# VectorE's work on the FFN input goes ahead of the rows between up and down, with two loads moved

## The chip, the cores and the metric

The kernel runs on one NeuronCore of a Trainium2 chip. The metric is device time in microseconds (us) of one execution. The engines that matter here are TensorE (PE), VectorE (DVE), ScalarE (ACT), GpSimd (POOL), and SyncE (SP), which issues nearly all DMAs. Each takes its instructions in the order in which the program lists them.

## The reference

The input x has 8 sequences of 1024 rows of 512 float32 numbers. One transformer layer is computed, in float32:

```
x1  = x  + attention(layernorm(x))      # 16 heads, low-rank queries, keys and values, rotary part, causal
out = x1 + ffn(layernorm(x1))
ffn(y) = down( silu(gate(y)) * up(y) )  # 512 -> 1408 -> 512
```

Each of the three linear maps of the FFN first rounds its input and its weights to a 4-bit grid: in blocks of 16 numbers, divided by the block's largest magnitude / 6, rounded to 0, 0.5, 1, 1.5, 2, 3, 4 or 6, and multiplied back. So `y` (the normalised x1) is rounded before gate and up, and `h = silu(gate) * up` before down.

## The kernel before

**Units and tiles.** The rows are cut into 16 units of 512 rows (two for each sequence) and each unit into 4 tiles of 128 rows, 64 tiles in all. Attention runs unit by unit: four groups of four heads, each with 3 (even units) or 7 (odd units) score steps. A score step is a set of score matmuls into the PSUM tile `sc_ps`, of which there is one, two exponentials on ScalarE (L597), a clamp of one half on VectorE (L612) and of the other on GpSimd (L615), masks on GpSimd (L619), and, one step later on PE, the matmuls with the values into `num`. VectorE also adds up the weights of the steps (L641). After a unit's attention comes the output projection (`po`), to which VectorE adds x (L772, tile `xo`); the sum x1 goes to a DRAM tile `mid`.

**The FFN as filler.** From the fifth unit on, pieces of the FFN are laid between the score steps, of tiles whose x1 has been stored. For tile n the pieces are: `fetch(n)` (load x1 into `y`, L786), `begin(n)` (layer norm and rounding of y, on VectorE), `turned(n)` (PE turns y, L212, and ScalarE copies it into `yT`), `gate(n, 0..2)` and `up(n, 0..2)` (chunks of 512, 512 and 384 columns), and `down(n)` (11 matmuls into `pd`). `down(n - 2)` stands between gate and up of tile n. For most of the kernel the pattern repeats every two units, that is every ten tiles, about 522 us; below, a tile's type is its number's last digit. The last tiles run after all attention has ended.

**Rows between up and down.** ScalarE copies gate's sums into a tile `h` (L142; two buffers), applies silu, and VectorE multiplies by up's sums (L831). `quantize` then makes the passes that round h: the largest magnitude of each block (L254), six small instructions for the scales (L259 to L264), and for each chunk L281 (divide), L289 and L292 (find the step), L295 twice (round), L277 (multiply back) and a transpose of blocks (L218). These passes are called rows below. Then 16 DMAs on SP (`move_blocks`, L230) put the blocks into `hT` (one buffer), which `down` reads. The y of a tile gets the same passes without the transpose, from 128x512 numbers. The tiles `y`, `sc`, `rs` (scales) and `m` (step) have one buffer each.

**PSUM banks.** All PE results but `sc_ps` and `num` go through three banks in turn (`bank`, pool `ps_t`): gate's and up's `pg`, the turned y `pt`, `pd`, `po`, and the projections `pp`, `pr`, `pf`, `pk`, `pq`, `pqr`, `pv`, `den`. A bank is written again when ScalarE or VectorE has read it.

**Order.** The Python code keeps a model clock (`Clock`) and writes the order of PE, VectorE, ScalarE and SP by it. VectorE's work that is not urgent goes into two queues, `soon` (attention) and `later` (FFN), and `fill` lays jobs from them where the model has VectorE idle before an instruction that waits for PE or ScalarE. `need(key)` lays everything in a queue up to the last job with that key: `turned(n)` needs y of n, `gate(n, 0)` needs h of n - 2. `later` is first in, first out, so y of tile n + 1 comes after whatever of h stands there. DMAs held in `sent` go out when the model clock passes their time or when they are asked for; stores ask before each `fetch`.

```
def gate(n, k):
    if k == 0:
        clk.need(("h", n - 2))
        clk.sent_by_now(("h", n - 2))
        hs[n] = p2.tile([P, FF], F32, tag="h", name="h")
```

Of the kernel before, what the change touches and what calls it, by code (L numbers as in the profile page):

```python
# [11 lines left out]
F32 = mybir.dt.float32  # L12
U32 = mybir.dt.uint32
AF = mybir.ActivationFunctionType
ALU = mybir.AluOpType
# [3 lines left out]
P = 128  # L19
B, S, D = 8, 1024, 512  # L20
# [7 lines left out]
NDC = D // P  # L28
NFC = FF // P
BLK = 16  # L30
# [12 lines left out]
def tile_mla_then_fp4_ffn(  # L43
# [17 lines left out]
    nc = tc.nc  # L61
    const = ctx.enter_context(tc.tile_pool(name="const", bufs=1))
    p1 = ctx.enter_context(tc.tile_pool(name="p1", bufs=1))
# [15 lines left out]
    class Clock:  # L79
# [4 lines left out]
        soon, later = deque(), deque()  # L84
# [14 lines left out]
                job[1]()  # L99

        def lay(self, q):
            cost, run, _, ready = q.popleft()
            self.dve = max(self.dve, ready) + cost
            run()

# [36 lines left out]
        on_act(0.1 + 0.0009 * src.free_size(), lambda: nc.scalar.copy(dst, src))  # L142

    def slack(cost, run, key, soon=False, ready=0.0):
        (clk.soon if soon else clk.later).append((cost, run, key, ready))

    ident = const.tile([P, P], F32, name="ident")
    make_identity(nc, ident)
# [68 lines left out]
    def turn_blocks(part, key, soon=False):  # L217
        slack(0.72, lambda: nc.vector.transpose(part, part), key, soon)  # L218
# [24 lines left out]
    BY_PE = (4 * 2 * B - 1,)  # L243


    def quantize(q, width, key):
        nb = width // BLK
        q3 = q.rearrange("p (b k) -> p b k", k=BLK)
        got = {}

        def amax():
            got["sc"] = sc = p1.tile([P, 88], F32, tag="sc", name="sc")[:, :nb]
            got["rs"] = rs = p1.tile([P, 88], F32, tag="rs", name="rs")[:, :nb]
            nc.vector.tensor_reduce(rs, q3, AX.X, ALU.max, apply_absolute_value=True)  # L254

        def scales():
            sc, rs = got["sc"], got["rs"]

            nc.vector.tensor_scalar(sc, rs, 1.0 / 6.0, None, ALU.mult)  # L259
            nc.vector.scalar_tensor_tensor(rs, sc, -4.0, rs, ALU.mult, ALU.add)  # L260
            nc.vector.scalar_tensor_tensor(rs, sc, -2.0, rs, ALU.mult, ALU.add)
            nc.vector.scalar_tensor_tensor(sc, rs, 1.0 / 6.0, sc, ALU.mult, ALU.add)
            nc.vector.tensor_scalar(sc, sc, 1e-12, None, ALU.max)
            nc.vector.reciprocal(rs, sc)  # L264

        slack(0.06 + 0.0011 * width, amax, key)
        slack(1.1 + 0.008 * nb, scales, key)
        for o in range(0, width, 512):
            step = min(512, width - o)
            part, bl = q[:, o : o + step], slice(o // BLK, (o + step) // BLK)  # L270
            nbl = step // BLK
            part3 = part.rearrange("p (b k) -> p b k", k=BLK)

            def times(which, part3=part3, bl=bl, nbl=nbl):
                by = got[which][:, bl].unsqueeze(2).to_broadcast([P, nbl, BLK])
                if which == "sc":
                    nc.vector.tensor_tensor(part3, part3, by, ALU.mult)  # L277
                else:


                    nc.vector.scalar_tensor_tensor(  # L281
                        part3, part3, BELOW_ONE, by, ALU.mult, ALU.mult
                    )

            def steps(part=part, step=step):
                got["m"] = m = p1.tile([P, 512], F32, tag="m", name="m")[:, :step]
                nc.vector.tensor_scalar(  # L289
                    m.bitcast(U32), part.bitcast(U32), EXP_MASK, None, ALU.bitwise_and  # L290
                )
                nc.vector.tensor_scalar(m, m, 1.0, MAGIC, ALU.max, ALU.mult)  # L292

            def to_grid(op, part=part):
                nc.vector.tensor_tensor(part, part, got["m"], op)  # L295

            pass_cost = 0.06 + 0.00125 * step
            slack(pass_cost, lambda f=times: f("rs"), key)
            slack(1.2 * pass_cost, steps, key)
            slack(pass_cost, lambda f=to_grid: f(ALU.add), key)  # L300
            slack(pass_cost, lambda f=to_grid: f(ALU.subtract), key)
            slack(pass_cost, lambda f=times: f("sc"), key)
            if key[0] == "h" and key[1] not in BY_PE:
                turn_blocks(part, key)


    def weight_pieces():
# [45 lines left out]
    def normed(xt, key):  # L353
        got = {}

        def stats():
            pool, tag = (small, "nx") if key[0] == "x" else (p1, "ny")
            own = pool.tile([P, 10], F32, tag=tag, name=tag)
            st, ve = own[:, 0:6], own[:, 8:9]
            got["mv"], got["rstd"] = mv, rstd = own[:, 6:8], own[:, 9:10]  # L360
            nc.vector.bn_stats(st, xt)
            nc.vector.bn_aggr(mv, st)
            nc.vector.tensor_scalar(ve, mv[:, 1:2], EPS, None, ALU.add)
            nc.gpsimd.tensor_tensor(rstd, ve, neg_half, ALU.pow)

        def scaled():
            nc.vector.tensor_scalar(
                xt, xt, got["mv"][:, 0:1], got["rstd"], ALU.subtract, ALU.mult
            )

        return [(0.9, stats, key), (0.5, scaled, key)]

    def begin_norms(jobs, soon=False):

        parts = [normed(*job) for job in jobs]
        for k in range(2):
            for part in parts:
                slack(*part[k], soon)
# [399 lines left out]


    tiles = [(u, t) for u in range(2 * B) for t in range(NT)]  # L780
    ys, hs, ends = {}, {}, {}

    def fetch(n):
        clk.sent_by_now("store")
        ys[n] = p1.tile([P, D], F32, tag="y", name=f"y_{n}")
        nc.sync.dma_start(out=ys[n], in_=mids[tiles[n]])  # L786

    def begin(n):
        begin_norms([(ys[n], ("y", n))])
        quantize(ys[n], D, ("y", n))  # L790

    def hidden(n, w, off, width):
        pg = bank("pg")[:, :width]
# [9 lines left out]

    def turned(n):
        clk.need(("y", n))
        yT = p2.tile([P, NDC, P], F32, tag="yT", name="yT")
        turn(ys[n], yT, NDC)
        ys[n] = yT

# [32 lines left out]
    def hidden_turned(n, done=None):  # L842

        if n in BY_PE:
            return
        if n > 0 and n - 1 not in used:
            waits[n] = clk.dve
            return
        h = hs.pop(n)

        def make():
            clk.sent_by_now("store")
            ends[n] = p3.tile([P, D], F32, tag="xo", name=f"xr_{n}")
            nc.sync.dma_start(out=ends[n], in_=mids.pop(tiles[n]))
            hTs[n] = p1.tile([P, NFC, P], F32, tag="hT", name="hT")
            return hTs[n]

        move_blocks(h, make, ("h", n), clk.dve if n == 0 or done is None else max(done, clk.pe))

    def down(n):  # L860
        clk.need(("h", n))
        if n in BY_PE:
            ends[n] = p3.tile([P, D], F32, tag="xo", name=f"xr_{n}")
            nc.sync.dma_start(out=ends[n], in_=mids.pop(tiles[n]))
            hTs[n] = p1.tile([P, NFC, P], F32, tag="hT", name="hT")
            for off, width in FCH:
                f0, c = off // P, width // P
                turn(hs[n][:, off : off + width], hTs[n][:, f0 : f0 + c, :], c)
            hs.pop(n)
        else:  # L870
            arrived(("h", n))
        hT = hTs[n]
        pd = bank("pd")
        for i in range(NFC):
            mm(pd, lhsT=hT[:, i, :], rhs=wd_T[:, i, :], start=(i == 0), stop=(i == NFC - 1))
        hTs.pop(n)
        used.add(n)
        if n + 1 in waits:
            hidden_turned(n + 1, waits.pop(n + 1))
        xt = ends.pop(n)  # L880
        on_dve(0.7, clk.pe + 0.3, lambda: nc.vector.tensor_tensor(xt, pd, xt, ALU.add))
        u, t = tiles[n]
        b, rows = rows_of(u, t)
        clk.send(clk.dve, lambda: nc.sync.dma_start(out=out[b, rows, :], in_=xt), "store")

    def ffn_pieces():

        last = len(tiles) - 1
        yield 4.0, 0, lambda: fetch(0)
        yield 10.0, 0, lambda: begin(0)  # L890
        yield 1.0, 0, lambda: turned(0)
        for n in range(last + 1):
            for k in range(3):
                yield (3.4, 3.4, 2.6)[k], n, lambda n=n, k=k: gate(n, k)
                if k < 2 and n < last:
                    yield 0.0, n + 1, lambda n=n, f=(fetch, begin)[k]: f(n + 1)
            if n > 1:
                yield 9.9, n, lambda n=n: down(n - 2)
            for k in range(3):
                yield (3.4, 3.4, 2.6)[k], n, lambda n=n, k=k: up(n, k)  # L900
                if k == 1 and n < last:
                    yield 0.5, n + 1, lambda n=n: turned(n + 1)
        for n in (last - 1, last):
            yield 9.9, last, lambda n=n: down(n)

# [135 lines left out]
```

## Time and profile before

| | |
|---|---|
| median of 3 runs | 3835.66 us (3835.64 to 3838.62) |
| profiled execution: time, span | 3835.01 us, 3833.3 us |
| mean granted TensorE clock | 0.974 |
| busy: PE, DVE, ACT, POOL | 3559.1 (93%), 2873.8 (75%), 1145.5 (30%), 651.2 (17%) us |
| PE's matmuls of gate, up, down | 630.6, 669.2, 622.9 us |

How to read it: PE, DVE and so on are busy times of one profiled execution. A group of instructions is named by the line that records it, so that all matmuls carry L129, and what distinguishes them is the tile they write: `pg`, `pd`, `pt` and so on. A 128x512 matmul appears as two instructions. A wait is listed as who waited, for whom, the total, the number of times and the longest. In a timeline, a row has its start, its length, engine, line, operation, tiles, sizes, the number of instructions, and in brackets the idle time before it with what ended it. A clock of 1.00 or 0.50 is the TensorE clock that was granted in a stretch.

### The profile page before, as it was taken

Reading aid. Unit: us, or ns where it says so; the run is one execution under the profiler, and the core shown is the slowest. Engines: PE = TensorE matmul, PEld = TensorE weight load, DVE = VectorE, ACT = ScalarE, POOL = GpSimd, SP = SyncE. Lnnn points to the kernel's source line nnn. Section 1 sums busy time; section 2 is a strip of 40 time slices with the busy share of each in tenths; the row PEclk is TensorE's granted clock in tenths of the full one; section 3 lists DMA queues with packets and bytes.
Section 4 is the critical chain, followed back from the end, with each engine's and each line's share of the span. In section 5 each row is a group of like instructions: output and inputs, shape, how many; then the busy total and the mean of one; then the engine's idle time right before and its main releaser. Section 6 shows DMA issues by size and latency. Waiting matters only on the chain. (4 is left out here: it accounts for less than half of the span.)

```text
span 3833.3 us, 45944 instructions
## 1 busy us (share of the span) xinstructions
PE 3559.1 (93%) x17119; PEld 1551.5 (40%) x17119; DVE 2873.8 (75%) x5024; ACT 1145.5 (30%) x1473; POOL 651.2 (17%) x838
## 2 busy tenths in 40 slices
PE   6998989999999998999999999989999999998898
PEld 3333334443444443344434444433444344433343
DVE  5886937777878777777778687776878786777776
ACT  2343433332323222232323233322323222232210
POOL 2233321111111111111111111111211111111100
PEclk9999999999999999999999999999999999999999
DMA  3212211311122211222111222112221113211221
GB/s 76 64 37 69 81 36 30 76 38 38 38 63 46 70 38 32 54 56 69 38 38 38 69 54 59 34 32 70 47 68 31 38 38 75 51 41 29 46 61 40
DMA packets 577038, 192.47 MB, mean 50 GB/s; under 512 B 514864, under 2 KB 515888, under 8 KB 576816
## 3 DMA queue, kind: packets, MB, share of 16 engines
q1 hardware_dynamic: 568512, 187.36, 21.0%
q10 hardware_dynamic: 8304, 2.18, 0.3%
q8 instruction: 136, 2.23, 0.2%
q14 instruction: 86, 0.70, 0.1%
HBM read 94.72 MB, written 33.55 MB: 33 GB/s over the span
## 5 line engine op out<-in xcount | busy, mean ns | idle before, releaser
L597 ACT ACTIVATE pT<-sc_ps 128x1024 f32<-128x1024 f32 (+1 forms) x640 | 566.1, 936 | 1174.6 <-PE sc_ps L129 964.6
L129 PE MATMUL pg<-wu_T,yT 128*128 128x512 f32 (+1 forms) x1536 | 669.2, 584 | 3.8 <-DVE xo L772 3.8
L129 PE MATMUL pg<-wg_T,yT 128*128 128x512 f32 (+1 forms) x1536 | 630.6, 561 | 0.7 <-ACT yT L214 0.7
L129 PE MATMUL pd<-wd_T,hT 128*128 128x512 f32 x1408 | 622.9, 598 | 4.4 <-DVE rs L264 4.4
L615 POOL TENSOR_SCALAR pT<-pT 128x1024 f32<-128x1024 f32 (+1 forms) x320 | 342.1, 1069 | 1065.4 <-ACT pT L597 847.6
L619 POOL TENSOR_SCALAR_AFFINE_SELECT pT<-pT 128x256 f32<-128x256 f32 (+1 forms) x384 | 233.4, 608 | 1462.6 <-DVE pT L612 1184.0
L641 DVE TENSOR_TENSOR pT<-pT 128x1024 f32<-128x1024 f32 (+3 forms) x528 | 472.7, 920 | 3.9 <-POOL pT L619 0.6
L129 PEld LDWEIGHTS pg<-wu_T,yT 128*128 128x128 f32 x1536 | 296.9, 200 | 333.9 <-issue 274.4
L129 PEld LDWEIGHTS pg<-wg_T,yT 128*128 128x128 f32 x1536 | 288.8, 190 | 326.1 <-issue 248.9
L129 PEld LDWEIGHTS pd<-wd_T,hT 128*128 128x128 f32 x1408 | 266.3, 191 | 345.5 <-issue 327.6
L612 DVE TENSOR_SCALAR pT<-pT 128x1024 f32<-128x1024 f32 (+1 forms) x320 | 205.0, 641 | 248.0 <-ACT pT L597 246.9
L129 PE MATMUL sc_ps<-qc,kT 32*128 32x512 f32 (+3 forms) x3072 | 343.5, 532 | 9.1 <-ACT pT L597 9.0
L129 PE MATMUL num<-pT,v 128*32 128x512 f32 (+3 forms) x3072 | 326.1, 501 | 5.6 <-POOL pT L619 5.2
L129 PE MATMUL sc_ps<-qr,kr 32*128 32x512 f32 (+3 forms) x3072 | 309.8, 488 | 4.2 <-DVE qr L533 4.2
L142 ACT COPY h<-pg 128x512 f32<-128x512 f32 (+1 forms) x192 | 105.7, 551 | 609.3 <-PE pg L129 580.6
L831 DVE TENSOR_TENSOR h<-pg,h 128x512 f32<-128x512 f32 (+1 forms) x192 | 123.1, 642 | 218.8 <-PE pg L129 208.3
L295 DVE TENSOR_TENSOR h<-h,m 128x512 f32<-128x512 f32 (+1 forms) x384 | 257.3, 670 | 11.8
L129 PE MATMUL po<-wo,aT 128*128 128x512 f32 x512 | 226.2, 600 | 30.9 <-DMA wo<-in_w_o_dram 27.9
L129 PEld LDWEIGHTS sc_ps<-qc,kT 32*128 32x128 f32 x3072 | 115.9, 186 | 226.8 <-issue 154.8
L212 PE MATMUL pt<-ident,y 128*128 128x128 f32 x256 | 48.2, 319 | 168.5 <-DVE y L277 158.1
L772 DVE TENSOR_TENSOR xo<-po,xo 128x512 f32<-128x512 f32 x64 | 44.1, 688 | 202.5 <-DMA xo<-in_x_dram 113.4
L129 PEld LDWEIGHTS sc_ps<-qr,kr 32*128 32x128 f32 x3072 | 147.3, 188 | 109.9 <-issue 85.5
(103 smaller groups left out, 3473.3 us busy)
## 6 DMA issues: line engine op xcount, KB each, us to landing
hT<-h SPq DMA_DIRECT2D x1008, 44.0 KB, 2.1
xo<-in_x_dram SPq DMA_DIRECT2D x64, 256.0 KB, 2.9
wo<-in_w_o_dram SPq DMA_DIRECT2D x16, 1024.0 KB, 5.2
mid<-xo SPq DMA_DIRECT2D x64, 256.0 KB, 2.8
y<-mid SPq DMA_DIRECT2D x64, 256.0 KB, 2.7
xr<-mid SPq DMA_DIRECT2D x64, 256.0 KB, 2.8
out_dram<-xr SPq DMA_DIRECT2D x64, 256.0 KB, 2.0
xp<-in_x_dram SPq DMA_DIRECT2D x30, 512.0 KB, 4.0
```

What stands on the lines that cost most here:

```text
L129: nc.tensor.matmul(dst, **kw)
L142: on_act(0.1 + 0.0009 * src.free_size(), lambda: nc.scalar.copy(dst, src))
L212: nc.tensor.transpose(pt[:, i, :], src[:, i * P : (i + 1) * P], ident)
L295: nc.vector.tensor_tensor(part, part, got["m"], op)
L597: lambda: nc.scalar.activation(part, sc[:, 2 * k : 2 * k + 2, :cols], AF.Exp, scale=SM_SCALE),
L612: lambda: nc.vector.tensor_scalar(part, part, E_HI, E_LO, ALU.min, ALU.max),
L615: nc.gpsimd.tensor_scalar(part, part, E_HI, E_LO, ALU.min, ALU.max)
L619: nc.gpsimd.affine_select(out=diag, in_=diag, pattern=[[0, 2], [0, len(segs)], [1, P]], compare_op=ALU.is_ge, fill=0.0, base=0, channel_mu ...
L641: lambda a=whole, b=part: nc.vector.tensor_tensor(a, a, b, ALU.add),
L772: on_dve(0.7, clk.pe + 0.3, lambda: nc.vector.tensor_tensor(xt, po, xt, ALU.add))
L831: lambda: nc.vector.tensor_tensor(h, pg, h, ALU.mult),
```

## The change

Jobs in VectorE's queues get a fifth field that says whether another tile's passes may be put ahead of them; it is false for the two roundings (L295), since the single tile `m` is in use there. `begin(n)` no longer appends: it puts the layer norm and all rounding passes of y, in one run, at the first place in `later` where that is allowed, so ahead of the rows of h. The scales of y, which so far shared `sc` and `rs` with h, are kept in two stretches of the tile `yT` that y itself will be copied into later. `begin(n + 1)` is called after `gate(n, 0)` and not after `gate(n, 1)`; `fetch(n + 2)` follows `turned(n + 1)`, so that this load stands ahead of `up(n, 2)` and `gate(n + 1, 0)`, where it stood behind both. `turned` sets the model's PE clock to VectorE's if that is later. The load of x1 for the last addition (`xr`) moves from ahead of the 16 moves to `down`. No instruction is added or removed on any engine; the order of PE is the same up to the last two units.

```
-        slack(0.06 + 0.0011 * width, amax, key)
...
+            jobs.append((1.2 * pass_cost, steps, key, True))
+            jobs.append((pass_cost, lambda f=to_grid: f(ALU.add), key, False))
+            jobs.append((pass_cost, lambda f=to_grid: f(ALU.subtract), key, False))
+            jobs.append((pass_cost, lambda f=times: f("sc"), key, True))
...
+    def ahead_of_rows(jobs):
+
+        q = clk.later
+        at = next((i for i, x in enumerate(q) if x[4]), len(q))
+        for job in reversed(jobs):
+            q.insert(at, (*job, 0.0, True))
...
     def begin(n):
-        begin_norms([(ys[n], ("y", n))])
-        quantize(ys[n], D, ("y", n))
+
+        yTs[n] = yT = p2.tile([P, NDC, P], F32, tag="yT", name="yT")
+        jobs = normed(ys[n], ("y", n))
+        scales_in = lambda: (yT[:, 0, : D // BLK], yT[:, 1, : D // BLK])
+        jobs += [x[:3] for x in quantize_jobs(ys[n], D, ("y", n), scales_in)]
+        ahead_of_rows(jobs)
...
     def turned(n):
         clk.need(("y", n))
-        yT = p2.tile([P, NDC, P], F32, tag="yT", name="yT")
+        clk.pe = max(clk.pe, clk.dve)
+        yT = yTs.pop(n)
...
         def make():
-            clk.sent_by_now("store")
-            ends[n] = p3.tile([P, D], F32, tag="xo", name=f"xr_{n}")
-            nc.sync.dma_start(out=ends[n], in_=mids.pop(tiles[n]))
             hTs[n] = p1.tile([P, NFC, P], F32, tag="hT", name="hT")
...
     def down(n):
         clk.need(("h", n))
+        clk.sent_by_now("store")
+        ends[n] = p3.tile([P, D], F32, tag="xo", name=f"xr_{n}")
+        nc.sync.dma_start(out=ends[n], in_=mids.pop(tiles[n]))
...
+        yield 0.0, 1, lambda: fetch(1)
         for n in range(last + 1):
             for k in range(3):
                 yield (3.4, 3.4, 2.6)[k], n, lambda n=n, k=k: gate(n, k)
-                if k < 2 and n < last:
-                    yield 0.0, n + 1, lambda n=n, f=(fetch, begin)[k]: f(n + 1)
+                if k == 0 and n < last:
+                    yield 0.0, n + 1, lambda n=n: begin(n + 1)
...
                 if k == 1 and n < last:
                     yield 0.5, n + 1, lambda n=n: turned(n + 1)
+                    if n + 1 < last:
+                        yield 0.0, n + 2, lambda n=n: fetch(n + 2)
```

More of the change, by code (lines that the diff above doesn't have):

```diff
@@ L101, in lay @@
         def lay(self, q):
-            cost, run, _, ready = q.popleft()
+            cost, run, _, ready, _ = q.popleft()
             self.dve = max(self.dve, ready) + cost
@@ L144, in slack @@
     def slack(cost, run, key, soon=False, ready=0.0):
-        (clk.soon if soon else clk.later).append((cost, run, key, ready))
+        (clk.soon if soon else clk.later).append((cost, run, key, ready, True))
+    def ahead_of_rows(jobs):
[3 more added lines that the diff above has]
+            q.insert(at, (*job, 0.0, True))
     ident = const.tile([P, P], F32, name="ident")
@@ L243, in tile_mla_then_fp4_ffn, with quantize_jobs @@
     BY_PE = (4 * 2 * B - 1,)
-    def quantize(q, width, key):
+    def quantize_jobs(q, width, key, scales_in):
         nb = width // BLK
         q3 = q.rearrange("p (b k) -> p b k", k=BLK)
-        got = {}
+        got, jobs = {}, []
         def amax():
-            got["sc"] = sc = p1.tile([P, 88], F32, tag="sc", name="sc")[:, :nb]
-            got["rs"] = rs = p1.tile([P, 88], F32, tag="rs", name="rs")[:, :nb]
+            got["sc"], got["rs"] = sc, rs = scales_in()
             nc.vector.tensor_reduce(rs, q3, AX.X, ALU.max, apply_absolute_value=True)
@@ L264, in scales @@
             nc.vector.reciprocal(rs, sc)
-        slack(0.06 + 0.0011 * width, amax, key)
-        slack(1.1 + 0.008 * nb, scales, key)
+        jobs.append((0.06 + 0.0011 * width, amax, key, True))
+        jobs.append((1.1 + 0.008 * nb, scales, key, True))
         for o in range(0, width, 512):
@@ L297, in quantize, with own @@
             pass_cost = 0.06 + 0.00125 * step
[L298 to L302, printed above, removed]
-            if key[0] == "h" and key[1] not in BY_PE:
-                turn_blocks(part, key)
+            jobs.append((pass_cost, lambda f=times: f("rs"), key, True))
+            jobs.append((1.2 * pass_cost, steps, key, True))
+            jobs.append((pass_cost, lambda f=to_grid: f(ALU.add), key, False))
+            jobs.append((pass_cost, lambda f=to_grid: f(ALU.subtract), key, False))
+            jobs.append((pass_cost, lambda f=times: f("sc"), key, True))
+            if key[0] == "h" and key[1] not in BY_PE:
+                jobs.append((0.72, lambda p=part: nc.vector.transpose(p, p), key, True))
+        return jobs
+    def quantize(q, width, key):
+        def own():
+            return [p1.tile([P, 88], F32, tag=x, name=x)[:, : width // BLK] for x in ("sc", "rs")]
+        for cost, run, k, free in quantize_jobs(q, width, key, own):
+            clk.later.append((cost, run, k, 0.0, free))
     def weight_pieces():
@@ L780, in tile_mla_then_fp4_ffn @@
     tiles = [(u, t) for u in range(2 * B) for t in range(NT)]
-    ys, hs, ends = {}, {}, {}
+    ys, yTs, hs, ends = {}, {}, {}, {}
     def fetch(n):
@@ L861, in down @@
         clk.need(("h", n))
+        clk.sent_by_now("store")
+        ends[n] = p3.tile([P, D], F32, tag="xo", name=f"xr_{n}")
+        nc.sync.dma_start(out=ends[n], in_=mids.pop(tiles[n]))
         if n in BY_PE:
-            ends[n] = p3.tile([P, D], F32, tag="xo", name=f"xr_{n}")
-            nc.sync.dma_start(out=ends[n], in_=mids.pop(tiles[n]))
             hTs[n] = p1.tile([P, NFC, P], F32, tag="hT", name="hT")
```

## The prediction

> **What bounds the kernel now.** The page comes first: PE is busy 93% of the span, so a change counts by what it does to PE's remaining 270 us of idle time and to the rate at which PE works.
>
> ```profile
> PE 3559.1 (93%) x17119; PEld 1551.5 (40%) x17119; DVE 2873.8 (75%) x5024; ACT 1145.5 (30%) x1473; POOL 651.2 (17%) x838
> ```
>
> Then the list of PE's waits and the cores' clock. The turn of y waits for y's last pass 40 times, 158.1 us in all; no other wait is near it. The turn also waits for L772, the addition of x after the output projection: the bank is late.
>
> ```profile
> PE pt L212 <- DVE y L277: 158.1, 40, 10.0
> PE pt L212 <- DVE xo L772: 10.4, 6, 2.6
> PE pg L129 <- DVE xo L772: 3.8, 4, 1.7
> core 0: 3833.3 us, clock 0.974
> ```
>
> A clock of 0.974 with steps of 0.50 alone means 2 x 0.026 x 3833.3 = 199 us at half rate. The table by windows shows where: behind the waits for y (start and end, length, busy times by engine, clock).
>
> ```profile
> 1941.20:1944.60 3.40, 3.40 (x8) 1.94 (x7) 0.00 (x0) 0.59 (x1) 0.00 (x0) 0.50 0.39 60
> 1989.00:1995.80 6.80, 4.83 (x28) 2.13 (x28) 1.76 (x3) 1.39 (x3) 0.00 (x0) 0.50 0.22 52
> ```
>
> The waits that end at 1940.84 (2.19 us) and 1990.97 (7.37 us) stand just before these. Last, PE's timeline at a tile of type 6 (26), beside ScalarE, VectorE and SP there; the rows of VectorE and SP are the last rows of h of tile 24 and its moves.
>
> ```profile
> 1893.80 1.12 PE L212 MATMUL pt<-ident,y 128*128 128x128 f32 x4 [5.69 <-DVE y L277]
> 1894.70 3.80 PE L129 MATMUL pg<-wu_T,yT 128*128 128x384 f32 x8
> 1898.34 3.60 PE L129 MATMUL pg<-wg_T,yT 128*128 128x512 f32 x8
> 1901.77 1.89 PE L129 MATMUL pp<-xnT,wdq 128*128 128x256 f32 x8
> 1903.59 0.64 PE L129 MATMUL pf<-krp,fold_sb 128*32 128x256 f32 x8
> ...
> 1906.66 1.12 PE L129 MATMUL pqr<-cq,wqr 128*128 128x512 f32 x2
> ```
> ```profile
> 1901.97 0.59 ACT L142 COPY h<-pg 128x512 f32<-128x512 f32 x1 [6.44 <-PE pg L129]
> ```
> ```profile
> 1867.29 0.36 DVE L289 TENSOR_SCALAR m<-h 128x384 uint32<-128x384 uint32 x1
> 1867.68 0.36 DVE L292 TENSOR_SCALAR m<-m 128x384 f32<-128x384 f32 x1
> 1868.08 1.15 DVE L295 TENSOR_TENSOR h<-h,m 128x384 f32<-128x384 f32 x2
> ...
> 1872.02 0.55 DVE L277 TENSOR_TENSOR h<-h,sc 128x384 f32<-128x384 f32 x1
> 1872.60 0.58 DVE L218 STREAM_TRANSPOSE h<-h 128x384 f32<-128x384 f32 x1
> ```
> ```profile
> 1873.31 11.43 SPq L230 DMA_DIRECT2D hT<-h  x16
> ```
>
> The rows of h end at 1873.2, the moves land at 1886.1, and down starts on them at 1916.0: 30 us of slack. In types 0 to 9 this slack is 19 to 50 us. So y is late while h is early.
>
> **What it removes.** I laid VectorE's durations in the changed order, each instruction starting no sooner than the PE, ScalarE or DMA row that it waits for, with PE's rows closed up by the waits removed. y's passes (about 8 us) come one to three score steps sooner, and their last one ends 12 to 55 us ahead of the turn. Only tile 0 is as before: nothing stands between its load and its turn, 9.6 us. Removed: 158.1 - 9.6 = 148.5 us.
>
> L772 waited because the load of x for the projection's second tile stood behind 16 moves on SP; in the new order it stands ahead of them, and PE's 10.4 + 3.8 = 14.2 us go.
>
> ```profile
> 1252.02 10.49 SPq L230 DMA_DIRECT2D hT<-h  x16
> 1262.57 0.60 SPq L182 DMA_DIRECT2D xo<-in_x_dram  x1
> ```
>
> Half clock: between 560 and 3640 us the clock's records have 150.2 us at 0.50, all behind waits for y; 52.6 of them PE was idle anyway (in the second window above 1.97 of 6.80), and 97.6 it worked at half rate, which loses 48.8 us. Gain in all: 148.5 + 14.2 + 48.8 = 211.5 us.
>
> The load of x1 beside down costs nothing: it goes out once SP is past the moves and has 9.6 us of matmuls to land in (2.8 us). y's scales in yT cost nothing: that buffer's last reader, up of the tile two before, is past.
>
> **What it adds: the h buffer.** No instruction is new, but the rows of h now end when `gate(n, 0)` forces them. The row that tells what this costs is ScalarE's wait for the moves, today only in the last tiles:
>
> ```profile
> ACT h L142 <- DMA hT<-h: 19.3, 3, 7.0
> ```
>
> h has two buffers, so the copy of gate's first chunk of tile n must wait until the moves have read h of n - 2. Type 6 by the rows above: up's last chunk ends on PE at 1898.5, its product (L831, 0.56) at 1899.1; in the new order a whole last chunk of h follows, 0.36 + 0.36 + 1.15 + 0.55 + 0.58 = 3.0, to 1902.1. Sixteen moves at 0.65 us and 2.1 us to land make 11.9: 1914.0. ScalarE's copy, which today starts at 1901.97, ends at 1914.6. PE has two more banks, which pp and pf take; pqr needs the first again at 1906.7 and waits 7.9 us. Queued behind the copy on ScalarE are the copies of pp and pf and two exponentials; their followers have 8 us of slack and more once PE itself stands.
>
> The same sum for the other types gives copies late by 3.7 (type 2), 5.7 (5), 10.0 (7), 6.8 (8) and 2.0 us (0), but there the third bank is asked for later: PE waits 0.4 in type 2, 1.3 in type 8, nothing in 5, 7 and 0. One more: in type 5 y's load stands behind 32 moves on SP, VectorE reaches y some 8 us before it lands, and the clamp behind y is late for its `num` matmuls by 2 us. Sum for ten tiles 7.8 + 1.3 + 0.4 + 2.0 = 11.5, and by the 7.37 us row a wait of that length loses (4.83 / 2 =) 2.4 us of clock: 13.9. Five times: 69.5.
>
> A wait of 2 us has its nearest rows in those of 2.17 to 2.26: two of three are followed by a half-clock stretch of 3.4 us, worth 1.7, the third, as at 2041.0, by none. So the clock cost of the 2.0 us wait lies between 0 and 1.7; I take two thirds, five times: 5.7 us. The Trainium skill, "TensorE: Matmul & The Clock Gate", section "HAM oscillation — how this bites in real kernels", has the clock fall only after idle gaps of more than about 3.4 us. The trace disagrees, with half clock at 1941.2 after 2.19 us; by that rule these 5.7 us would be nothing and the forecast 3729.
>
> Start: h of tile 0 goes behind y of 2, so the copy of gate(2, 0) is 12.4 us late and PE, two groups on, waits 9.0; with the clock 11.4. End: in the last two units PE's order itself changes; in tiles 56, 57 and 58 a score step or `den` stands where the late copy counts, 1.0, 8.4 and 5.7 us, the last load of `wo` has 4 us less cover, and two long waits cost 4.8 of clock: 24. Costs in all: 69.5 + 5.7 + 11.4 + 24 = 110.6.
>
> The profiled execution took 3835.0, so 3835.0 - 211.5 + 110.6 = 3734.1; the median of the runs is 0.65 above it: 3735.
>
> **Bounds.** Each new wait could be nil (the bank asked for later than I have it) or be as long as the copy is late. The first end takes all costs away, 3624; the second is the last rival. The h wait of type 6 is nearest to rows, the end section furthest. The forecast's own range is 3690 to 3775: costs between 65 and 150.
>
> **Rivals.** *The buffer is hidden* (0.2): ScalarE is busy 30%, and if PE's rows shift so that rows of h end earlier against gate, only the start and a few us remain: 3624 + 20 = 3645. For it: VectorE is idle 25%. Against it: the 11.9 us of moves are longer than the 8.2 us from the product to pqr, wherever VectorE stands.
>
> *The load stays late* (0.13): the projection's additions do not come sooner, and y's load of type 5 lands another 6 us later, as now, behind both sets of moves. Then the clamp there is 8 us late, not 2: 5 x (6 + 2.4) = 42, and the 14.2 us stay: 3735 + 56 = 3791.
>
> *ScalarE passes every late copy on to PE* (0.07): if behind the copy the exponentials, not the banks, hold PE, each round of ten tiles costs all of 3.7 + 5.7 + 11.9 + 10.0 + 6.8 + 2.0 = 40 us, six rounds 241, and the half clock stays: 3835.7 - 162.7 + 241 = 3914, slower. It decides from 27 us a round on (162.7 / 6). Against it: in types 5 and 7 the next scores start after the late exponentials would have ended.
>
> That the change does nothing is ruled out by the new order itself.
>
> **Numbers.** Forecast 0.6, rivals 0.2, 0.13 and 0.07. The range 3640 to 3795 leaves out the last rival and the tails. No change is told from about 0.2% (8 us) on: faster 0.92, same 0.01, slower 0.07.
>
> **What would show it.** PE's wait for y L277 falls from 158.1 to about 10 us; the clock rises to about 0.985; ScalarE's wait for the moves (L142) grows to over 100 us; PE waits some 7.9 us before pqr in tiles 6, 16, 26, 36, 46. If y's wait stays above 50 us, or PE's waits behind L142 pass 160 us, the prediction is wrong.

## The result and the profile after

| | before | after |
|---|---|---|
| median | 3836.0 us (3835.64 to 3838.62) | 3807.17 us (3796.05 to 3811.5) |
| profiled execution: span, clock | 3833.3 us, 0.974 | 3806.9 us, 0.971 |
| PE idle after 540 us | 204.9 us | 174.9 us |
| PE time lost to half clock after 540 us | 56.9 us | 62.3 us |

The ratio is 0.9919 with a 95% interval of 0.9897 to 0.9941: faster by 29 us where 101 were forecast, and outside the range of 3640 to 3795. The idle time is the sum of PE's waits of more than 0.15 us; the loss to half clock is half of the time that PE worked at a clock of 0.50. From about 540 us on, pieces of the FFN stand between the score steps.

First the busy times on the page, and the cores' clock, of the changed kernel:

```profile
PE 3562.8 (94%) x17119; PEld 1554.5 (41%) x17119; DVE 2856.5 (75%) x5024; ACT 1137.3 (30%) x1473; POOL 667.6 (18%) x838
```
```profile
core 0: 3806.9 us, clock 0.971
```

The clock was to rise to 0.985 and fell by 0.003 in the profiled executions; over all executions measured it is 0.970 to 0.974 before and 0.971 to 0.975 after, so it hardly changed. The list of waits (who waited, for whom, total, times, longest) shows what took the place of the waits for y:

```profile
ACT h L142 <- DMA hT<-h: 370.4, 28, 26.5
DVE ny L376 <- DMA y<-mid: 63.2, 9, 10.3
PE pqr L129 <- ACT h L142: 42.1, 5, 9.2
PE num L129 <- POOL pT L634: 36.5, 20, 5.5
PE sc_ps L129 <- ACT pT L612: 25.4, 22, 7.8
PE pp L129 <- ACT h L142: 13.8, 5, 3.5
PE pp L129 <- DVE krp L467: 11.4, 6, 3.8
PE pt L219 <- DVE y L284: 9.6, 1, 9.6
```

(L212 and L277 of before are L219 and L284 here, L230 is L237, the exponentials L597 are L612, the clamps L612 and L615 are L627 and L630, the masks L619 are L634, L772 is L787, L786 is L801, L831 is L851.) The waits for y are down from 158.1 to 9.6, and those for the addition of x are gone. New are ScalarE's 370 us of waiting for the moves, PE's waits behind that, and, after 540 us, `num` for GpSimd's mask, which stood nowhere there before.

Tile 26, type 6, in the timeline of the changed kernel: PE, ScalarE, VectorE and SP (start, length, line, tiles; in brackets the idle time before and what ended it).

```profile
1887.36 3.60 PE L129 MATMUL pg<-wg_T,yT 128*128 128x512 f32 x8
...
1894.69 1.07 PE L129 MATMUL num<-pT,v 128*32 128x512 f32 x8
1904.01 2.07 PE L129 MATMUL pqr<-cq,wqr 128*128 128x512 f32 x2 [8.26 <-ACT h L142]
```
```profile
1903.37 0.59 ACT L142 COPY h<-pg 128x512 f32<-128x512 f32 x1 [17.75 <-DMA hT<-h]
```
```profile
1887.56 0.56 DVE L851 TENSOR_TENSOR h<-pg,h 128x384 f32<-128x384 f32 x1
...
1890.60 0.58 DVE L311 STREAM_TRANSPOSE h<-h 128x384 f32<-128x384 f32 x1
```
```profile
1891.25 10.51 SPq L237 DMA_DIRECT2D hT<-h  x16
```

This is the chain of the prediction: product, 3.1 us of rows, 12.1 us from the first move to ScalarE's copy, and PE without a bank for 8.26 us. (The sum for the rows leaves out the divide of the last chunk; in the run it lies ahead of the product, at 1885.51, and so costs nothing here.) The chain that was not sized right is the one at type 5. SP, VectorE and PE there:

```profile
1260.92 10.85 SPq L237 DMA_DIRECT2D hT<-h  x16
1271.88 0.55 SPq L789 DMA_DIRECT2D mid<-xo  x1
1272.47 11.26 SPq L237 DMA_DIRECT2D xnT<-xp  x16
1283.83 0.54 SPq L801 DMA_DIRECT2D y<-mid  x1
```
```profile
1286.84 0.69 DVE L376 BATCH_NORM_STATS2 ny<-y 128x6 f32<-128x512 f32 x1 [10.35 <-DMA y<-mid]
...
1311.86 0.52 DVE L627 TENSOR_SCALAR pT<-pT 128x768 f32<-128x768 f32 x1
```
```profile
1313.39 0.64 PE L129 MATMUL num<-pT,v 128*32 128x128 f32 x4 [5.50 <-POOL pT L634]
1315.02 1.50 PE L129 MATMUL num<-pT,v 128*32 128x128 f32 x12 [0.98 <-POOL pT L634]
```

Two sets of 16 moves stand ahead of y's load on SP, those of h and those of the attention's input `xnT`. VectorE stands 10.35 us at y, since y is first in its queue, and from there to the clamp it is idle for only 0.67 us: 25 us later the clamp is still late, GpSimd's mask after it too, and PE waits 5.50 + 0.98 us. Last, what the clock does behind a wait of 3.79 + 0.98 us at 1830.5, of 8.26 us at 1904.0, and of 4.76 us at 2124.6 (start and end, length, busy times by engine, clock, DMA share, GB/s):

```profile
1829.00:1835.80 6.80, 4.33 (x19) 1.93 (x20) 6.59 (x11) 1.62 (x3) 3.52 (x4) 0.50 0.04 13
1900.70:1907.50 6.80, 3.49 (x4) 1.51 (x5) 1.90 (x4) 2.56 (x5) 1.39 (x3) 0.50 0.33 64
2122.60:2129.40 6.80, 4.75 (x6) 2.18 (x7) 2.79 (x6) 0.00 (x0) 0.00 (x0) 0.50 0.43 91
```

All three bring 6.80 us at half clock, and the shorter waits lose more by it (4.33 / 2 and 4.75 / 2 against 3.49 / 2), because PE works through more of the stretch. (Behind the other four waits of 8.2 to 9.2 us before `pqr` the stretch is 10.2 us long, but then more of it lies in the wait.)

### The profile page after: what moved, and what is told of

Read it like the earlier page. It is cut to its first block, busy times and chain, and to the rows that moved or that the text cites. A ratio compares the mean times of both kernels' runs of the same rounds, so it can differ in the third digit from the quotient of the medians.

```text
span 3806.9 us, 45954 instructions
## 1 busy us (share of the span) xinstructions
PE 3562.8 (94%) x17119; PEld 1554.5 (41%) x17119; DVE 2856.5 (75%) x5024; ACT 1137.3 (30%) x1473; POOL 667.6 (18%) x838
## 4 chain that ended last, share of the span: by engine, by line
PE 60%; DVE 13%; SPq 6%; issue 4%; ACT 2%; DMA 2%; POOL 1%; ACTq 0%; DVEq 0%; POOLq 0%
PE pg L129 22%; PE pd L129 12%; PE sc_ps L129 8%; SPq L237 6%; PE po L129 5%; PE num L129 4%; PE pp L129 2%; DVE pT L656 2%; DVE h L302 2%; PE den L129 1%; DMA hT<-h 1%; PE pv L129 1%; PE pk L129 1%; PE pqr L129 1%; DVE h L284 1%
## 5 line engine op out<-in xcount | busy, mean ns | idle before, releaser
L612 ACT ACTIVATE pT<-sc_ps 128x1024 f32<-128x1024 f32 (+1 forms) x640 | 567.3, 940 | 1130.0 <-PE sc_ps L129 1029.9
L129 PE MATMUL pg<-wu_T,yT 128*128 128x512 f32 (+1 forms) x1536 | 649.9, 570 | 0.7 <-ACT yT L221 0.7
L129 PE MATMUL pg<-wg_T,yT 128*128 128x512 f32 (+1 forms) x1536 | 638.9, 567 | 2.3 <-ACT h L142 1.6
L630 POOL TENSOR_SCALAR pT<-pT 128x1024 f32<-128x1024 f32 (+1 forms) x320 | 349.2, 1091 | 1061.6 <-ACT pT L612 723.6
L634 POOL TENSOR_SCALAR_AFFINE_SELECT pT<-pT 128x256 f32<-128x256 f32 (+1 forms) x384 | 238.9, 622 | 1583.8 <-DVE pT L627 1315.3
L656 DVE TENSOR_TENSOR pT<-pT 128x1024 f32<-128x1024 f32 (+3 forms) x528 | 463.8, 904 | 3.7 <-POOL pT L634 0.6
L627 DVE TENSOR_SCALAR pT<-pT 128x1024 f32<-128x1024 f32 (+1 forms) x320 | 202.9, 634 | 329.9 <-ACT pT L612 328.8
L129 PEld LDWEIGHTS pg<-wu_T,yT 128*128 128x128 f32 x1536 | 287.2, 193 | 325.0 <-issue 260.9
L142 ACT COPY h<-pg 128x512 f32<-128x512 f32 (+1 forms) x192 | 102.4, 554 | 785.6 <-DMA hT<-h 370.4
L129 PE MATMUL po<-wo,aT 128*128 128x512 f32 x512 | 238.1, 625 | 33.6 <-DMA wo<-in_w_o_dram 29.9
L851 DVE TENSOR_TENSOR h<-pg,h 128x512 f32<-128x512 f32 (+1 forms) x192 | 122.7, 639 | 139.9 <-PE pg L129 135.6
L129 PEld LDWEIGHTS num<-pT,v 128*32 128x32 f32 x3072 | 69.1, 109 | 250.5 <-issue 135.4
L129 PEld LDWEIGHTS po<-wo,aT 128*128 128x128 f32 x512 | 102.1, 201 | 167.2 <-issue 124.0
```

What stands on the lines that cost most here:

```text
L129: nc.tensor.matmul(dst, **kw)
L612: lambda: nc.scalar.activation(part, sc[:, 2 * k : 2 * k + 2, :cols], AF.Exp, scale=SM_SCALE),
L627: lambda: nc.vector.tensor_scalar(part, part, E_HI, E_LO, ALU.min, ALU.max),
L630: nc.gpsimd.tensor_scalar(part, part, E_HI, E_LO, ALU.min, ALU.max)
L634: nc.gpsimd.affine_select(out=diag, in_=diag, pattern=[[0, 2], [0, len(segs)], [1, P]], compare_op=ALU.is_ge, fill=0.0, base=0, channel_mu ...
L656: lambda a=whole, b=part: nc.vector.tensor_tensor(a, a, b, ALU.add),
```

## The experiments

Three questions are asked: how much the late load of y costs, how much the two `h` buffers cost, and what each part of the change is worth. Ratios are to the kernel before. Idle time and half-clock loss are those after 540 us.

**The load of y on another queue.**

```
 def fetch(n):
...
-    nc.sync.dma_start(out=ys[n], in_=mids[tiles[n]])
+    nc.scalar.dma_start(out=ys[n], in_=mids[tiles[n]])
```

> Edit: y's loads are issued by ScalarE, right behind its copy of the turned y, and no longer by SP behind 32 moves. Theory (the load of type 5 is late because of its place in SP's queue; VectorE stands at y in order, the clamp behind it and then num are late): VectorE's wait for the load (63.2 us) falls below 10, PE's num waits after 540 us (31.4) below 5, and five half-clock stretches (14 us of loss) go: 3807 - 26 - 14 = about 3767. Rival (the 16 DMA engines are full of the moves' small packets, so that another queue does not bring the load sooner): no change, 3800 to 3812. A third way: ScalarE itself stands at the issue, and the exponentials behind it are late: slower than 3812.

Measured: 3746.95 us, ratio 0.976 (0.9745 to 0.9774), 60 us below the changed kernel. In the timeline ScalarE issues the load with its copy of the turned y, without waiting for the moves on SP; in the list of waits `num` has only short waits left:

```profile
1261.01 0.33 ACTq L801 DMA_DIRECT2D y<-mid  x1
```
```profile
PE num L129 <- POOL pT L634: 7.2, 9, 1.5
PE pqr L129 <- ACT h L142: 42.0, 5, 8.8
```

The theory holds, and the effect is larger than expected: VectorE no longer stands at y, and the clamp starts 0.9 us after the last of its score matmuls, where it started 10.3 us after it. Idle time falls by 37.7 us (174.9 to 137.2) and the half-clock loss by 23.7 (62.3 to 38.6). Of the latter 13.9 stood behind the five `num` waits, and 2.6 behind a wait of 3.6 us near the end that is gone too. Most of the rest is that some other waits of 2 to 4 us were this time followed by no half clock. The orders of PE's and VectorE's work are those of the changed kernel: the place of one DMA in each tile was worth twice what the whole change brought.

**The rows of h sooner.**

```
 def turned(n):
     clk.need(("y", n))
     clk.pe = max(clk.pe, clk.dve)
     yT = yTs.pop(n)
     turn(ys[n], yT, NDC)
+    clk.need(("h", n - 2))
```

> Edit: turned(n) also lays the rows of h(n - 2) that are left, behind y's passes and ahead of the product of up(n - 1, 2). Theory (the two h buffers hold ScalarE's copy, and each PE wait of 2 us or more brings a half-clock stretch of its own): PE's waits for ScalarE's h copies (pqr 42.1 us in 5 waits, pp 13.8 in 5) go to under 8 us, and eight half-clock stretches that stood behind them (16 us of loss) go: 3807 - 48 - 16 = about 3743. The load of wo, which stands behind the same moves on SP, comes sooner too and may add 10 us. Rival (the rows only change places: laid ahead of the product they hold that product and the clamps behind it, and PE waits there instead): 3800 to 3815, with new PE waits for VectorE's product or for the clamp.

Measured: 3802.1 us, 0.9905 (0.989 to 0.992): the rival's time, though not by the waits that it named. The waits for the moves shrink little, and PE's waits for the load of `wo` grow from 29.9 to 50.5 us; beside them `den` waits 7.5 us. The list of waits, gate's first matmul of tile 26 on PE, and the moves of tile 24 in SP's timeline:

```profile
PE po L129 <- DMA wo<-in_w_o_dram: 50.5, 9, 12.6
PE pqr L129 <- ACT h L142: 33.2, 5, 7.3
```
```profile
1879.45 3.60 PE L129 MATMUL pg<-wg_T,yT 128*128 128x512 f32 x8
1881.58 10.49 SPq L237 DMA_DIRECT2D hT<-h  x16
```

In the changed kernel the moves begin 3.9 us after gate's first matmul (1891.25 - 1887.36), here 2.1 us after it (1881.58 - 1879.45). VectorE works without a gap from 1873.6 to 1885.7 us here, and laying the rows earlier in the order ends them only 1.8 us earlier. The moves still take 12 us, so the `pqr` waits lose 1.8 us each (42.1 to 33.2 in five).

**Both.** 

> Both edits together. Theory: the two causes are separate, so the gains add: 3807 - 64 - 40 = about 3703. Rival (either wait is covered by the other): as the better of the two alone, 3743.

Measured: 3748.99 us, 0.977 (0.9753 to 0.9786). It is what the load brings alone, not the 3703 of the theory; the rows add nothing, since PE's waits for `wo` rise from 31.0 to 45.0 us and `den` waits 7.5 us.

**The priority alone.** `fetch`, `begin` and the load of x1 for the last addition go back to their places of before:

```
-        yield 0.0, 1, lambda: fetch(1)
...
-                if k == 0 and n < last:
-                    yield 0.0, n + 1, lambda n=n: begin(n + 1)
+                if k < 2 and n < last:
+                    yield 0.0, n + 1, lambda n=n, f=(fetch, begin)[k]: f(n + 1)
...
-                    if n + 1 < last:
-                        yield 0.0, n + 2, lambda n=n: fetch(n + 2)
...
     def make():
+        clk.sent_by_now("store")
+        ends[n] = p3.tile([P, D], F32, tag="xo", name=f"xr_{n}")
+        nc.sync.dma_start(out=ends[n], in_=mids.pop(tiles[n]))
```

> The change with its priority alone: fetch, begin and the load of x1 for the last addition stand where they stood before the change. Theory (load stays late): the additions after the projection are late as before the change (14.2 us of PE waits for them), and y of type 5 lands some 6 us later than in the changed kernel, so the num waits grow from about 5 to 11 us each: 3807 + 14 + 30 = about 3851, slower than the kernel before. Rival (the places of the loads hardly count beside the priority): 3800 to 3815.

Measured: 3890.24 us, 1.0133 (1.0118 to 1.0148), slower than before, and 39 us more than expected, for another reason than expected. The `num` waits in type 5 did not grow to 11 us (the longest is 6.3), and few waits for the addition of x came back (3.2 us of 14.2). The list of waits names what was missed:

```profile
DVE ny L376 <- DMA y<-mid: 174.1, 18, 12.6
PE pg L129 <- DVE xr L901: 29.2, 5, 5.8
```

With y first in VectorE's queue and its load later still, VectorE stands 18 times at y, and the last addition (`xr`) behind it holds a bank: PE's waits for it are 53 us in all (before `pg`, `pt` and `pv`) where the changed kernel has 11. I had counted the clamps behind y and not the additions.

**All but the priority.**

```
 def ahead_of_rows(jobs):
     q = clk.later
-    at = next((i for i, x in enumerate(q) if x[4]), len(q))
+    at = len(q)
```

> The change without its priority: y's jobs go to the end of VectorE's queue; begin a group sooner, the loads' new places and the scales in yT stay. Theory (the gain is the priority's; the loads' places only take away the waits for the addition of x): PE's wait for y stays at 130 to 158 us, the waits for L787 (14.2) go, no waits for ScalarE's h copies: 3836 - 14 - 5 = about 3817. Rival (the loads' places bring the gain, since y is begun sooner by them): y's wait falls below 80 us, and the time is below that of the full change, 3807.

Measured: 3742.16 us, 0.9747 (0.9731 to 0.9763). Without the priority the change is 65 us faster than with it. The rival had the sign right (the loads' places bring a gain, and the time falls below 3807), but it put the waits for y below 80 us; nothing foresaw the size. In the list of waits y still holds PE, but 24 times and not 40, and nothing new stands beside it:

```profile
PE pt L219 <- DVE y L284: 96.0, 24, 9.6
ACT h L142 <- DMA hT<-h: 4.3, 1, 4.3
```

So on the changed kernel the priority takes 86 us of waits for y away and brings 138 us of others: idle time rises from 122.8 to 174.9, half-clock loss from 51.4 to 62.3.

**A third buffer for h**, on the kernel with y's loads by ScalarE:

```
-    wqr = const.tile([P, NH, DH], F32, name="wqr")
+    wqr = wqc
...
-    hs[n] = p2.tile([P, FF], F32, tag="h", name="h")
+    hs[n] = p3.tile([P, FF], F32, tag="h", name="h")
```

(and in the same way `wuv` in `wuk`, `wdkv` in `wdq`). To make room, this kernel leaves out three weights and lets others stand in for them, so that its output is not the layer's; the number and the order of PE's and VectorE's instructions stay.

> On the kernel with y's loads issued by ScalarE (3747): h gets a third buffer. To free the room, w_uv, the rotary part of w_q and w_dkv are not loaded and w_uk, the other part of w_q and w_dq stand in for them; work and order on all engines stay the same. Theory (the copies of gate's first chunk wait for the moves only because h has two buffers): PE's waits for ScalarE's h copies (pqr 42.0, pp 13.7, sc_ps in the last units some 14, pd and pg 5) go, and with them 8 half-clock stretches behind pqr and pp and 2 behind sc_ps (20 us): 3747 - 72 - 20 = about 3655, near the 3645 at which the prediction put a hidden buffer. Rival (the exponentials on ScalarE or the late rows themselves hold PE next, for instance down waiting for the moves): half of it or less, 3700 to 3745.

Measured: 3611.5 us, 0.9407 (0.9393 to 0.9421), 135 us below 3747 and 44 below the theory's 3655. The cores' clock and the list of waits:

```profile
core 0: 3610.0 us, clock 0.991
```
```profile
ACT h L142 <- DMA hT<-h: 21.7, 4, 5.4
```

No wait of PE's matmuls for h copies is left on the list. Over the whole span PE's idle time falls from 204.1 to 96.8 us and the half-clock loss from 49.8 to 23.1. Not all of this is the late copy: part of it lies before the first turn of y (at 556 and 533 us), where no tile of the FFN has begun on PE; the next runs show how much.

**The third buffer in the changed kernel itself, and without the priority.** The same edit on the other two kernels.

> The changed kernel itself (y's loads on SP, 3807) with the third h buffer; as in the earlier run, w_uv, the rotary part of w_q and w_dkv are not loaded and others stand in. Theory (late load and buffer are two causes): the waits for ScalarE's h copies go, the num waits for y's late load (31 us and their half clock, some 60 us in all) stay: 3807 - 136 = about 3671. Rival (with the copy free, ScalarE and VectorE run early enough that the load's place is covered): about 3611, as with both.

> The change without its priority (3742), with the third h buffer and the same weights standing in. Theory (only the priority makes the rows of h late, so only with it does the buffer count): PE's waits for y (96 us) stay, and the time stays at 3730 to 3745; priority alone is then worth -65 with two buffers and some +70 with three. Rival (the third buffer brings a gain of its own, by an earlier gate): 3700 or less.

Measured: 3668.78 us, 0.9558 (0.9544 to 0.9572), and 3721.01 us, 0.9693 (0.9677 to 0.971). The first is as expected: the load still costs 57 us with three buffers, so load and buffer are two causes that add. The second kernel keeps its waits for y (96.0 us, 24 times) and gains 21 us, more than the theory had, but from the first turn of y on its idle time is unchanged (113 and 114 us): the 15.2 us of idle time that it loses lie before it (PE's wait of `pr` for `xnT` alone goes from 13.2 to 5.4, with three weights fewer to load). So 21 us come with this edit and not with the late copies; idle time and half-clock loss before the first turn of y fall by about as much in the other two pairs (22 and 23 us). The late copies then cost 135 - 21 = 114 us with y's loads on ScalarE and 138 - 21 = 117 on SP. Together:

| y's loads on SP | two buffers | three buffers |
|---|---|---|
| without the priority | 3742 | 3721 |
| with the priority | 3807 | 3669 |
| the priority is worth | -65 | +52 |

**Late moves on two queues**, again with two buffers and y's loads by ScalarE:

```
+                    (nc.scalar if clk.late and q % 2 else nc.sync).dma_start(
...
         clk.need(("h", n - 2))
+        clk.late = any(x[2] == ("h", n - 2) for x in clk.sent)
         clk.sent_by_now(("h", n - 2))
+        clk.late = False
```

> On the same kernel (3747): where the moves of h(n - 2) have not gone out by gate(n, 0), 14 tiles, ScalarE issues 8 of the 16, right ahead of its copy, which waits for them anyway. Theory (the moves are slow because SP's queue takes 0.65 us for each; the 16 DMA engines are less than half busy meanwhile): the moves take 5.2 + 1.4 us instead of 10.5 + 1.4, PE's pqr waits fall from 8.3 to about 3 each (42 to 16), the sc_ps waits of the last units by some 8, clock 3 to 6 us: about 3747 - 26 - 8 - 5 = 3708. Rival (the DMA engines are the limit, or ScalarE pays for the issues): no gain, 3740 to 3760.

> The two queues for late moves (7 tiles here) and, as in the earlier run, the rows of h(n - 2) laid in turned(n), on the kernel with y's loads issued by ScalarE. Theory: pqr waits start from 6.5 and lose 5.2: below 2 us each, so that they bring no half clock; about 3747 - 33 - 10 = 3704, or less if the load of wo no longer stands behind late moves. Rival (as in the earlier run, what the rows gain in one place is lost before po and den): no better than the two queues alone.

Measured: 3688.22 us, 0.9607 (0.9593 to 0.9621), and with the rows laid in `turned` 3702.75 us, 0.9648 (0.9633 to 0.9662). Tile 16 of the first in ScalarE's, SP's and PE's timelines:

```profile
1343.59 5.33 ACTq L238 DMA_DIRECT2D hT<-h  x8
1350.94 0.59 ACT L143 COPY h<-pg 128x512 f32<-128x512 f32 x1 [12.95 <-DMA hT<-h]
```
```profile
1343.69 5.56 SPq L238 DMA_DIRECT2D hT<-h  x8
```
```profile
1351.58 1.12 PE L130 MATMUL pqr<-cq,wqr 128*128 128x512 f32 x2 [3.45 <-ACT h L143]
```

The orders of PE's and VectorE's work are those of the run without the edit. Sixteen moves now land in 7.4 us (1343.59 to 1350.94), not 12.1, and the `pqr` waits fall from 42.0 to 19.2. The gain, 59 us, is 20 more than expected: the `pp` waits behind ScalarE's copy go altogether (13.7 us), the `sc_ps` waits after 540 us fall from 16.5 to 5.8, and `wo` comes sooner (16.1 to 8.9). Laying the rows sooner costs 15 us here: `pqr` falls to 10.2, but PE's waits for `wo` after 540 us rise from 8.9 to 33.3 and `den` waits 7.0.

**Three buffers with all weights in place.** Main lines of the edit, besides h in `p3` (`p5` is a pool of five buffers that holds what `kT0` and `kT1` held in six):

```
+                    got["own"] = whole[:, 480 : 480 + nbl]
+                    nc.vector.reciprocal(got["own"], got["rs"][:, bl])
...
+                own = yTs[key[1]][:, 2, 0:10]
...
+            krp = proj[u][2][:, g * 256 : (g + 1) * 256]
...
+            kT = p5.tile([P, U], F32, tag="kT", name=f"kT_{u}_{hq}")
...
+            rc = den
```

> The same as the run with three h buffers and y's loads by ScalarE (3611), with all weights in place. Room comes from: keys of both halves in one tag of five buffers, krp inside kr, the softmax quotient in den's PSUM bank (the four steps laid at once), y's statistics in yT, and for h and the weights no sc tile: its values are formed per chunk in m, so chunks are 480, 480 and 448 wide. Theory (none of that is on PE's path): 3605 to 3630. Rival (the bank of den, held 1.5 us longer, and three more small VectorE instructions a tile hold PE): 3630 to 3680.

Measured: 3653.62 us, 0.9516 (0.9502 to 0.953). It beats both kernels, by 154 us the changed one. It lies 42 us above the run with weights left out, in the rival's range, but not by the rival's mechanism: 38 of these 42 us lie before the first turn of y (at 570.3 us, against 532.7), and from there to the end the two kernels take 3080.7 and 3077.3 us, though VectorE has 57 us more work (2913.8 against 2856.5). Of the 38 some 21 are what leaving out the weights had brought; in the rest PE waits longer for the rounded weights (`wraw`, 15.2 us against 7.3) and before `num` (19.2 against 4.1). Which of the edits costs this was not taken apart.

## Why the prediction was wrong

**Right.** The gain's terms all came: the waits for y fell by 148.5 us, as worked out, and the 14.2 us of the addition of x went. The floor, all costs away, was 3624; the kernel with neither late load nor buffer wait took 3611.5, or 3632 with the 21 us that its edit brings in any order added back. The type 6 wait was put at 7.9 us (7.8 in the sum) and was 8.20 to 9.20, five times, 42.1 us against 39. The end was put at 1.0, 8.4 and 5.7 us, and PE waited 1.27, 7.78 and 6.75 there for its score bank. ScalarE's wait for the moves passed 100 us by far. The two signs that were to show the prediction wrong did not come (y's wait 9.6 us, PE's waits behind L142 63 in all): they watched the rivals and not the term that failed.

**The first mis-sized term: y's late load.** The step said "the clamp behind it is late for its `num` matmuls by 2 us". The load was late about as worked out (VectorE stood 10.35 us against 8), but the wait was 4.8 to 6.5 us each, 31.4 with a few smaller ones, not 10. VectorE has 0.67 us of idle time between y and that clamp, so nearly the whole delay reaches it: against the run with the load on another queue the clamp is 9.4 us later behind its scores, and the mask that PE waits for follows it. With its half clock the term was priced at 15.7 us and is worth 60, as that run shows.

**The second: the waits that were put at nearly nothing.** `pp` behind the late copy of type 8 was put at 1.3 us and waits 2.3 to 3.5 (13.8 in all); `pp` for `krp` in type 2 at 0.4 us, and waits 1.5 (11.4 with 3.8 at the start). New waits of PE sum to 132.7 us, not 85.6 (204.9 - 162.7 = 42.2 were to be left, and 174.9 are there). The prediction had laid VectorE's work out on PE's rows with all the old waits closed up; that a bank asked for at about the copy's end there was asked for earlier in the run is likely the reason, but it was not shown. The start went the other way: it was put at 9.0 us, and PE waits 3.8 and 1.6 there.

**The third: the clock.** The prediction took 48.8 us of half clock away and put 25 back, a net -24; measured is +5.4. It scaled the loss with the wait: 2.4 us for the longest, nothing for what it had at 1.3. But the change replaced 40 waits, of which 21 were of 1.8 to 2.3 us and 11 of those without half clock, by new ones of 2.2 to 9, nearly each with a stretch of its own, and a stretch of half clock loses about the same behind a wait of 4 us as behind one of 9 (last section). Behind `pqr` the loss is as forecast (10.0 us against 12). It is larger behind `num` (13.9 against 5.7), behind `pp` for the late copy (7.8 against nothing), and behind the waits for the projection `po`: before the change six of these, of 2.3 to 3.3 us, brought no half clock, now five of 2.9 to 4.9 us cost 11.5. The forecast had none of these but the last load of `wo`. The terms make up the miss of 72 us (3807 - 3735) to within 4: new waits 132.7 - 85.6 = 47, clock 5.4 + 24 = 29, in sum 76. (These are the two profiled executions; the clock of single executions of one kernel differs by up to 0.004, worth up to some 8 us.) By the runs, the late load was worth 60 us and the late copies 114, 174 in all, where the prediction had 110.6.

**The step above the terms.** The change was priced as a whole. The runs show that with two `h` buffers its parts have opposite signs: the earlier loads and the earlier begin, with y's scales in `yT`, are worth 94 us without the priority (3836 to 3742; these parts were not taken apart), and the priority on top of them costs 65. The prediction booked nearly all of the 211 us of gain to the priority and did not ask how much the loads bring without it. The rivals all kept the priority as the source of the gain. "The load stays late" (3791) came nearest, and in part by luck: its mechanism, VectorE standing at y with the clamps behind it, was there, in a smaller dose, but the 14.2 us that it kept went.

**The rule of the Trainium skill.** The page "TensorE: Matmul & The Clock Gate", section "HAM oscillation — how this bites in real kernels", has the clock fall only after gaps of more than about 3.4 us. By it the forecast would have been 3729, further off. Above 3.4 us the runs bear it out without exception; below, waits of 2.1 to 3.4 us brought half clock in 58 of 91 cases.

## What to carry to other kernels

A job that is put first in an in-order queue makes everything behind it wait for that job's input: before moving it up, check when its load lands and whether the engine has a gap to catch up in afterwards (here 0.67 us in 25). Price each part of a change alone and in pairs, because with one buffer fewer the same reordering can cost what it would otherwise bring (-65 us with two `h` buffers, +52 with three). Where waits halve the clock, count the waits that are long enough for it, here those from about 2.1 us on: besides its length one of them cost 1.0 to 2.5 us on average, by the table below.

## What the hardware showed

**Half clock goes by the number of waits.** For the 13 profiles of this case (both kernels and 11 experiments) all PE waits of at least 0.9 us after 540 us were taken that stand 12 us or more from the next such wait. A stretch at 0.50 counts where it begins between the start of the wait and 4.5 us after its end. The loss is half of the time that PE worked in the stretch, as a mean over all waits of the row.

| length of the wait, us | waits | with half clock | mean loss, us |
|---|---|---|---|
| 0.9 to 2.1 | 136 | 5 | 0.06 |
| 2.1 to 2.5 | 46 | 27 | 1.0 |
| 2.5 to 3.4 | 45 | 31 | 1.3 |
| 3.4 to 5 | 59 | 59 | 2.3 |
| 5 to 8.5 | 65 | 65 | 2.3 |
| over 8.5 | 18 | 18 | 2.5 |

The stretches last 3.4, 6.8, 10.2 or 13.7 us. Behind a long wait much of the stretch falls into the wait itself, and so the loss hardly grows. This is read from waits that came as they came; no run set the length of a wait on purpose.

**A second queue shortens a series of small DMAs.** The 16 moves of 44 KB start 0.66 us apart on SP's queue, and meanwhile the DMA engines are less than half busy (0.45 from 1892.0 to 1900.6 us of the changed kernel). On SP's and ScalarE's queues together they took 7.4 us and not 12.1. The Trainium skill, page "DMA: Bandwidth & Descriptors", section "Rules for kernel authors", says that spreading DMAs over issuing engines does not help bandwidth and only saves issue time. The trace agrees on the issue time, and here it was what PE waited for: 59 us of 3747. As long as one queue's issue was the limit, the second queue raised the rate too: the engines' share went from 0.45 to 0.75 and what they moved from 65 to 107 GB/s (1343.6 to 1350.9 us of the run with two queues).
